# Two graph layers on 64 graphs: an order of their own for the weights and the first three graphs, Wv x aw, the constant and the bias sum on TensorE, turned square matrices in halves

## The chip, the cores and the metric

The kernel runs on one core of one Trainium2 chip. The metric is the device time of one execution in microseconds (us), and several executions are summed up by their median. The five engines named here are PE (TensorE), DVE (VectorE), ACT (ScalarE), POOL (GpSimd) and SP (SyncE, which only issues DMAs here). Each executes its own instructions in program order and waits for the others through semaphores.

## What is computed

There are 64 graphs of 256 nodes with 512 features, all in float32. Each graph goes through two layers, each with a layer norm, a relu and a residual sum around it.

```python
def _L0_gnn_ref(x, adj, W):
    deg = jnp.sum(adj, axis=-1, keepdims=True)
    agg = jnp.einsum('bij,bjf->bif', adj, x) / jnp.maximum(deg, EPS)
    cat = jnp.concatenate([x, agg], axis=2)
    return jax.nn.relu(jnp.einsum('bnf,of->bno', cat, W))

def _L1_gnn_ref(X, A, Wv, bv, aw, ab, Wk, bk):
    Xw = X @ Wv + bv
    sj, si = Xw @ aw[:d, 0], Xw @ aw[d:, 0]
    e = leaky_relu(sj[:, None, :] + si[:, :, None] + ab[0], negative_slope=0.2)
    alpha = A * jnp.exp(e)
    transition = alpha / (jnp.sum(alpha, axis=-1, keepdims=True) + 1e-12)
    H, Xk = 0, X
    for k in range(3):
        H = H + Xk @ Wk[k] + bk[k]
        Xk = jnp.einsum('bij,bjd->bid', transition, Xk)
    return jax.nn.relu(H)

h = jnp.maximum(_layernorm(x), 0.0);  x = x + _L0_gnn_ref(h, adj, W)
h = jnp.maximum(_layernorm(x), 0.0);  x = x + _L1_gnn_ref(h, adj, Wv, bv, aw, ab, Wk, bk)
```

Since `sj` and `si` are linear in X, the kernel never forms `Xw`. It computes once the two vectors v = Wv x aw (one for each half of aw, 512 numbers each) and the constant c = bv x aw + ab. The three rows of bk only ever occur as their sum.

## The kernel before

**Stages.** One graph is worked on in twelve stages (the list `ORDER`): `prepare` normalises x and scales the adjacency rows by the degree; `prepared` brings both turned; `aggregate` multiplies adjacency by h; `layer0` multiplies by W and adds to x; `turn1` normalises again and forms sj and si; `transition` builds the transition matrix; `moved`, `once`, `inner`, `turned1` and `outer` do layer 1 with it and store the result. `once` and `inner` need the turned transition matrix, and `inner` the weight Wk[2]. Large products are done with seven block products instead of eight (functions `spread`, `step`, `main`), so each needs sums of blocks: those of operands are made by `pool_op` on POOL, those of results by `copy` (ACT), `plus` and `minus` (DVE), which read PSUM. `main` has an order: step 5, then 1, 6 and 7, whose results pile up in one bank and are read between, and then 2, 3 and 4.

**The turned matrices.** `put` turns 32 by 32 blocks on DVE and stores them to DRAM in four DMAs, and `get` loads the whole turned matrix in one (`dan` and `ant` for the adjacency, `dtt` and `tt` for the transition, `dh` with `h0t` and `h1t` for h). Turned this way, the nodes of the two halves alternate in a row, so a half is read with a stride of two elements (8 bytes). For graphs 0 and 1 (adjacency and h) and the last two (transition) `flip_on_pe` turns on PE instead. In `spread` (function `turned`) `ant`, `tt` and their sums `sa` and `st` are the streamed operand of 128x128 products; in `outer` `tt` is the stationary one.

**Weights.** W, Wv, Wk, the biases and aw come in through SP. `weights_l0` turns W on PE, block by block, and ACT and DVE copy the blocks out in turn; `combine` makes the four further forms of a weight (1024-wide sums). `weights_l1` forms v on DVE, where Wv rows are multiplied by a broadcast aw with a running sum (line 607, ten such passes with those for c at line 626), sends it to DRAM (`dv`, line 610) and loads it back broadcast to all partitions (`v_sb`, line 612). The rows of bk are loaded broadcast and summed on DVE.

**Order.** Nothing is scheduled while the kernel runs. Every operation is recorded with `plan.add` (engine, a cost, what it reads and writes) and gets a due time from the table `AT` by stage and place in the stage, plus graph number times `TURN` and an entry of `SHIFT` for the first five and last five graphs. `emit` sorts each engine's operations by due time and writes them out; the costs do not enter the program. So an engine's queue is fixed, and an instruction that waits holds everything behind it. In the queue of SP loads and stores of all stages stand in one line.

**Closed stream.** After `inner` of graph 0 PE goes over to a repeating pattern, in which `outer` of one graph, `aggregate` and `layer0` of the graph two on, and `once` and `inner` of the graph between are interleaved. It is called the stream below.

Of the kernel before, what the change touches and what calls it, by code (L numbers as in the profile page):

```python
# [9 lines left out]
FP = mybir.dt.float32  # L10
BF = mybir.dt.bfloat16
AF = mybir.ActivationFunctionType
ALU = mybir.AluOpType
# [9 lines left out]
EDGE = 5  # L23
TURN = 41.62
AT = {
    "aggregate": (-3.8, 0.1, -3.6, 5.6, -18.4, -16.1, 2.2, -2.0, 2.2, 3.7, 9.3, 4.8, 4.4, 4.5, 5.0, 5.2, 14.3, 6.9, 13.8, 12.7, 10.0, 17.0, 11.4,
        18.9, 21.4),
    "first": (-579.1, -953.8, -882.7, -935.3, -1158.8, -875.5, -1084.4, -1059.4, -1372.1, -1103.9, -1257.7, -1270.0, -1219.5, -1116.0, -1213.5,
        -1124.5, -1222.8, -734.4, -1039.8, -990.3, -891.0, -945.8, -621.6, -565.5, -688.7, -847.3, -687.6, -419.9, -454.2, -670.2, -638.5, -533.2,
        -493.0, -301.0, -425.6, -241.2, -378.7, -391.4, -136.3, -308.3, -102.8, -3.0, -445.1),  # L30
    "inner": (79.0, 79.2, 80.3, 81.6, 79.5, 80.6, 80.7, 81.2, 82.3, 83.4, 83.7, 85.5, 86.5, 81.3, 86.1, 90.2, 104.7),
    "layer0": (5.8, 7.8, 11.6, 13.8, 6.8, 7.1, 14.9, 10.1, 10.2, 18.2, 13.6, 13.8, 15.2, 15.6, 16.8, 21.0, 27.0, 15.4, 16.4, 16.9, 17.5, 17.6, 18.4,
        22.0, 24.8),
    "loads": (-98.9, -113.0),
    "moved": (61.9, 69.8, 70.0, 71.6, 71.8),
    "once": (48.3, 49.8, 42.7, 60.1, 61.5, 65.2, 74.5, 70.0, 65.7, 66.7, 69.9, 70.9, 75.2, 70.4, 77.7, 76.5, 72.3, 77.8, 77.8, 78.3, 79.3),
    "outer": (81.8, 94.7, 105.9, 107.5, 84.9, 86.5, 92.3, 94.9, 96.6, 98.4, 98.5, 101.7, 102.6, 104.5, 106.4, 110.8, 109.6, 110.9, 111.5, 114.5,
        116.8, 117.1, 119.3, 120.1, 120.3, 125.6, 118.0, 118.6, 134.3, 139.3, 141.1, 145.8),
    "prepare": (-80.0, -76.6, -71.5, -69.0, -55.5, -53.4, -55.5, -20.1, -17.1, -104.1, -102.8, -91.0, -83.1, -82.8, -22.8, -22.9, -16.9, -16.1,
        -16.2, -17.5, -77.8, -47.6, -76.7, -52.4, -52.1),  # L40
    "prepare_early": (-499.7, -495.0, -519.1, -455.0, -518.6, -498.1, -241.7, -264.2, -416.8, -347.6, -281.6, -123.2, -111.2, -155.7),
    "prepared": (-12.9, -36.0),
    "prepared_early": (-136.7, -57.2, -102.3, -120.6, -45.1, -43.2, -73.0, -34.9),
    "transition": (33.1, 43.1, 53.6, 53.3, 53.8, 52.7, 50.1, 50.7, 50.6, 51.4, 51.5, 59.2, 59.4, 54.2, 58.0, 58.7, 55.9, 57.4),
    "transition_late": (28.6, 33.0, 57.8, 64.4, 61.5, 63.2, 59.1, 60.6, 60.9, 62.7, 64.3, 71.2, 71.5, 66.0, 69.8, 75.9, 91.9),
    "turn1": (24.0, 24.4, 26.7, 27.0, 31.9, 33.7, 29.4, 35.2, 35.5, 31.5, 32.5, 32.8, 41.4, 46.7, 50.6, 44.2, 46.3, 52.8, 52.0, 50.8, 51.3),
    "turned1": (79.0,),
    "weights": (-241.4, -226.2, -416.0, -218.0, -259.6, -285.0, -147.1, -112.2, -407.3, -158.3, -411.9, -155.5, -223.9, -130.8, -612.2, -212.8,
        -230.2, -181.7, -278.5, -209.9, -293.2, -203.1, -159.6, -81.9, -54.5, -36.5, -27.6, -3.8, -59.7, -38.2, 50.4, 51.5, 103.2, 18.1, -112.2,
        -238.5, 28.7, 43.7, -3.3, 3.7, 11.4, 21.4, 38.9, 9.0, 28.9, 12.6),  # L50
}
SHIFT = {(name, g): shift for g, row in {
    -5: {"aggregate": 0.5, "inner": 3.5, "layer0": 0.9, "loads": 5.6, "moved": 1.1, "once": 2.0, "outer": 3.9, "prepare": -1.3, "prepared": 15.2, "transition": 1.9, "turn1": -0.8, "turned1": 7.3},
    -4: {"aggregate": 0.9, "inner": 6.7, "layer0": 0.4, "loads": -2.2, "moved": 5.9, "once": 4.1, "outer": 4.8, "prepare": -1.2, "prepared": 12.3, "transition": 3.5, "turn1": -0.3, "turned1": 8.8},
    -3: {"aggregate": 3.5, "inner": 12.6, "layer0": 4.8, "loads": 7.5, "moved": 10.5, "once": 11.1, "outer": 9.9, "prepare": 0.7, "prepared": 20.2, "transition": 9.1, "turn1": 4.4, "turned1": -6.4},
    -2: {"aggregate": 9.6, "inner": 32.0, "layer0": 9.6, "loads": 0.8, "moved": 17.6, "once": 29.5, "outer": 37.1, "prepare": 5.9, "prepared": 18.0, "transition_late": 4.8, "turn1": 8.9, "turned1": 15.9},
    -1: {"aggregate": 16.4, "inner": 72.9, "layer0": 23.3, "loads": -1.2, "moved": 44.0, "once": 57.0, "outer": 78.7, "prepare": 9.1, "prepared": 30.2, "transition_late": 36.7, "turn1": 22.8, "turned1": 20.1},
# [66 lines left out]
def gnn_two_layers(ctx: ExitStack, tc: tile.TileContext, x, adj, w0, wv, bv, aw, ab, wk, bk, out):  # L124
# [39 lines left out]
    TURNED_A = buf("turneda", [N // Q, Q, NC], 2)  # L164
    H0T, H1T = buf("h0t", [FC, P, NC], 1), buf("h1t", [FC, P, NC], 1)
    S0, S1 = buf("s0", [4, 2, P], 1), buf("s1", [4, 2, P], 1)
    ANT, TT = buf("ant", [NC, P, NC], 1), buf("tt", [NC, P, NC], 2)
    SA, ST = buf("sa", [4, P], 1), buf("st", [4, P], 2)
    AG, ZG = buf("ag", [7, 2, P], 1), buf("zg", [7, 2, P], 1)
    QF = buf("qf", [7, half], 1)  # L170
# [538 lines left out]
```

## Time and profile before

| what | value |
|---|---|
| median of 3 runs | 2637.4 us (2636.27 to 2637.7) |
| the profiled execution's own time | 2636.42 us |
| its span (first to last instruction) | 2634.6 us |
| PE busy | 2572.8 us, 13520 matmul instructions |
| DVE, POOL, ACT busy | 1498.9, 1463.5, 696.2 us |
| mean granted TensorE clock | 0.99 |
| data moved by DMA | 300.48 MB, mean 114 GB/s |
| first and last store of a graph issued | 171.4 us, 2630.7 us |
| tt from DRAM, issue to landing, median | 2.9 us |

All times in the profile count from the start of the span. A product of float32 shows as several matmul instructions ("x4" for two products). A line of the timeline gives the start, the length, the engine, the source line, the operation and its tiles (output, then inputs) with the number of merged instructions, and in brackets the idle time before it and what ended that. Where the profile names a line of a helper (296, 308, 311, 259), the tiles tell which stage it is.

### The profile page before, as it was taken

The numbers are of one execution on the slowest core, as the hardware profiler recorded it, in microseconds if no ns is written. First come the engines' busy times: TensorE is split into PE (matmuls) and PEld (weight loads), VectorE is DVE, ScalarE is ACT, GpSimd is POOL, SyncE is SP. The second block draws the span as 40 slices with busy tenths as digits, with TensorE's granted clock in tenths as the row PEclk, the third lists the DMA queues.
The fourth block names the chain that finished last, engine by engine and source line by source line (L and its number), as shares of the span: only waits on it lengthen the run. The fifth ranks groups of instructions, "written<-read, shape, count | busy, mean of one in ns | idle before, by whom it ended". The sixth has DMA issues, their size and how long they took to land.

```text
span 2634.6 us, 39436 instructions
## 1 busy us (share of the span) xinstructions
PE 2572.8 (98%) x13520; PEld 2309.4 (88%) x13520; DVE 1498.9 (57%) x3686; ACT 696.2 (26%) x1680; POOL 1463.5 (56%) x2317
## 2 busy tenths in 40 slices
PE   5799999999999999999999999999999999999998
PEld 4688999999999999999999999999999998998887
DVE  5656556556556556556556556555555555556543
ACT  2223222222322322222222222222222222222221
POOL 4555555556556556556556556556556556556542
PEclk8799999999999999999999999999999999999999
DMA  5445445445445455354454455354355454445421
GB/s 177 88 112 129 102 120 129 102 120 129 100 122 125 103 124 128 97 126 122 101 128 121 100 125 127 98 128 120 101 128 121 99 130 120 102 114 125 103 67 50
DMA packets 578568, 300.48 MB, mean 114 GB/s; under 512 B 419904, under 2 KB 543808, under 8 KB 578368
## 3 DMA queue, kind: packets, MB, share of 16 engines
q1 hardware_dynamic: 578368, 297.97, 45.8%
q8 instruction: 107, 1.75, 0.3%
q14 instruction: 93, 0.76, 0.1%
HBM read 165.68 MB, written 132.19 MB: 113 GB/s over the span
## 4 chain that ended last, share of the span: by engine, by line
PE 95%; DMA 2%; DVE 2%; ACT 1%; issue 1%; POOL 0%; SPq 0%; DVEq 0%; ACTq 0%; POOLq 0%
PE bank L296 95%; DMA qf<-in_L_gnn_Wk_dram 1%; DMA dv<-vc 0%; DMA a<-in_adj_dram 0%; DVE z L471 0%; DMA lq<-in_L_gnn_Wk_dram 0%; ACT an L407 0%; DMA x<-in_L_gnn_W_dram 0%; DVE qf L311 0%; DVE z L607 0%; DMA dan<-turneda 0%; DVE stats L208 0%; ACT qf L308 0%; DVE x L398 0%; ACT si L453 0%
## 5 line engine op out<-in xcount | busy, mean ns | idle before, releaser
L296 PE MATMUL bank<-l,s 128*128 128x256 f32 x2048 | 527.6, 380 | 3.3 <-DVE bank L311 2.3
L296 PE MATMUL bank<-l,zg 128*128 128x256 f32 x1792 | 459.6, 379 | 0.0
L296 PE MATMUL bank<-l,ag 128*128 128x256 f32 x1792 | 451.9, 380 | 2.3 <-ACT ag L308 2.3
L259 POOL TENSOR_TENSOR zg<-zg 128x256 f32<-128x256 f32 x192 | 138.5, 734 | 562.7 <-ACT zg L308 546.9
L296 PEld LDWEIGHTS bank<-l,s 128*128 128x128 f32 x2048 | 380.1, 191 | 51.1 <-issue 2.6
L296 PE MATMUL bank<-lq,zg 128*128 128x256 f32 x1792 | 399.0, 379 | 2.5 <-DVE zg L311 1.4
L296 PEld LDWEIGHTS bank<-lq,zg 128*128 128x128 f32 x1792 | 339.7, 190 | 51.2 <-DVE zg L311 2.5
L296 PEld LDWEIGHTS bank<-l,ag 128*128 128x128 f32 x1792 | 341.6, 191 | 48.9 <-ACT ag L308 2.8
L296 PEld LDWEIGHTS bank<-l,zg 128*128 128x128 f32 x1792 | 330.5, 189 | 39.5
L259 POOL TENSOR_TENSOR ag<-ag 128x256 f32<-128x256 f32 x192 | 150.6, 785 | 364.3 <-DVE ag L311 225.5
L398 DVE SCALAR_TENSOR_TENSOR x<-bank,x 128x512 f32<-128x512 f32 x256 | 173.8, 679 | 94.1 <-PE bank L296 88.7
L296 PE MATMUL bank<-l,h1t 128*128 128x256 f32 x780 | 202.2, 382 | 5.2 <-ACT bank L308 3.3
L449 DVE SCALAR_TENSOR_TENSOR z<-h1n,v_sb 128x512 f32<-128x512 f32 x256 | 189.5, 740 | 12.6 <-ACT h1n L215 3.9
L296 PE MATMUL bank<-l,h0t 128*128 128x256 f32 x756 | 194.7, 380 | 1.1 <-DVE bank L383 0.6
L311 DVE TENSOR_TENSOR mq<-bank,mq 128x256 f32<-128x256 f32 x128 | 54.2, 424 | 225.7 <-PE bank L296 225.7
L208 DVE BATCH_NORM_STATS2 stats<-x 128x6 f32<-128x512 f32 x256 | 176.0, 688 | 2.3
L308 ACT COPY bank<-bank 128x256 f32<-128x256 f32 x128 | 45.7, 357 | 496.2 <-DVE bank L389 382.8
L308 ACT COPY zg<-bank 128x256 f32<-128x256 f32 x128 | 47.6, 372 | 471.9 <-DVE zg L311 299.9
L296 PEld LDWEIGHTS bank<-l,h1t 128*128 128x128 f32 x780 | 147.9, 197 | 20.6 <-ACT bank L308 3.7
L296 PEld LDWEIGHTS bank<-l,h0t 128*128 128x128 f32 x756 | 143.2, 196 | 15.4 <-ACT m L308 1.2
L296 PE MATMUL bank<-qf,st 128*128 128x256 f32 x512 | 152.3, 379 | 0.0
L259 POOL TENSOR_TENSOR s<-s,h1t 128x256 f32<-128x256 f32 x195 | 144.6, 743 | 0.1
(123 smaller groups left out, 4182.1 us busy)
## 6 DMA issues: line engine op xcount, KB each, us to landing
dh<-turned SPq DMA_DIRECT2D x504, 128.0 KB, 3.1
x<-in_x_dram SPq DMA_DIRECT2D x64, 512.0 KB, 4.3
h1t<-dh SPq DMA_DIRECT2D x64, 512.0 KB, 5.5
out_dram<-x SPq DMA_DIRECT2D x64, 512.0 KB, 3.8
h0t<-dh SPq DMA_DIRECT2D x62, 512.0 KB, 4.7
a<-in_adj_dram SPq DMA_DIRECT2D x64, 256.0 KB, 3.3
dan<-turneda SPq DMA_DIRECT2D x248, 64.0 KB, 4.2
ant<-dan SPq DMA_DIRECT2D x62, 256.0 KB, 2.8
```

What stands on the lines that cost most here:

```text
L208: add("DVE", 0.67, lambda c=c: nc.vector.bn_stats(st[:, c, :], s[:, c, :]), [f"{sk}.{c}"], [f"{stk}.{c}"])
L259: add("POOL", cost, lambda: getattr(nc.gpsimd, f)(to, p, q), reads, [write])
L296: nc.tensor.matmul(ps, lhs, rhs, start=start, stop=True, skip_group_check=True)
L308: add("ACT", 0.37, lambda: nc.scalar.copy(dst, bank[b][:, cols]), [f"bank{b}"], dkeys)
L311: add("DVE", 0.43, lambda: nc.vector.tensor_add(dst, bank[b][:, cols], other), [f"bank{b}"] + okeys, dkeys)
L398: add("DVE", 0.69, lambda c=c: nc.vector.scalar_tensor_tensor(t[:, c, :], bank[banks[1 + c]], 0.0, t[:, c, :], op0=ALU.max, op1=ALU.add), ...
L449: add("DVE", 0.85, lambda s=s, c=c: nc.vector.scalar_tensor_tensor(scr.rearrange("p c n -> p (c n)"), h[:, c, :], 1.0, v_sb[:, s, :], op0= ...
```

## The change

- **Order.** `AT` is a new table throughout, with two decimals. Graphs 0, 1 and 2 (`OWN = 3`) have due times of their own for every stage instead of a common table and a shift; the shifts remain for the last four graphs, and `moved` has a late form for the last two. `TURN` is the same. The costs in `add`, which emit nothing, are changed too. `warm` emits nothing, as `WARM` is 0.
- **Loads.** Graph 0's x comes in two halves, and its adjacency is the second load of all; W's four blocks follow, with graph 1's x and adjacency between them, then layer 1's weights.
- **v, c and the bias sum.** aw is loaded as 1024 single elements to a column per partition and spread by ACT to 128 columns; Wv is turned on PE (16 turns, copied out by ACT), and PE multiplies. The result is broadcast to all partitions as it comes. c is 8 products of one column, the bias sum one product with ones. The broadcast loads, the passes on DVE and the way through DRAM are gone.
- **Halves.** `ant` and `tt` hold the two halves of a row one after the other. The load goes to a new tile `raw`, and ACT copies it over (`even`). The turns on PE are copied straight into the new layout.
- **Engines.** For graphs 0 and 1 the sums for `ag`, `zg`, `qf`, `sa` and `st` go from POOL to DVE. Of W's blocks ACT copies twelve of sixteen instead of eight; ACT alone copies out the turned h.

```diff
-EDGE = 5
+EDGE = 4
+OWN = 3
+WARM = 0
...
-    ANT, TT = buf("ant", [NC, P, NC], 1), buf("tt", [NC, P, NC], 2)
+    ANT, TT = buf("ant", [NC, NC, P], 1), buf("tt", [NC, NC, P], 2)
+    RAW = buf("raw", [NC, P, NC], 2)
...
+    def even(raw, to):
+        (r, rk), (t, tk) = raw, to
+        add("ACT", 0.62, lambda: nc.scalar.copy(t, r.rearrange("p k n c -> p k c n")), [rk, rk + "'"], [tk, tk + "'"])
...
-                (nc.scalar.copy if c else nc.vector.tensor_copy)(t[:, :, :, c], pt[:, :n, :])
+                (nc.scalar.copy if c or width == F else nc.vector.tensor_copy)(t[:, :, :, c] if width == F else t[:, :, c], pt[:, :n, :])
...
     def pool_op(f, cost, to, p, q, reads, write):
-        add("POOL", cost, lambda: getattr(nc.gpsimd, f)(to, p, q), reads, [write])
+        if plan.graph < 2 and write[:2] in ("ag", "zg", "qf", "sa", "st"):
+            add("DVE", 0.45 if cost > 0.6 else 0.3, lambda: getattr(nc.vector, f)(to, p, q), reads, [write], port=True)
+        else:
+            add("POOL", cost, lambda: getattr(nc.gpsimd, f)(to, p, q), reads, [write])
...
     def left_of_t(tt, s):
-        a11, a12, a21, a22 = (t[:, k, :, c] for c in range(2) for k in range(2))
+        a11, a12, a21, a22 = (t[:, k, c] for c in range(2) for k in range(2))
...
-            get(N, of(D["an"], g), of(ANT, g))
+            get(N, of(D["an"], g), RAW[0])
+            even(RAW[0], of(ANT, g))
...
-            get(N, of(D["tt"], g), of(TT, g))
+            get(N, of(D["tt"], g), RAW[1])
+            even(RAW[1], of(TT, g))
...
-                        (nc.scalar.copy if oc % 2 else nc.vector.tensor_copy)(to[:, 2 * side : 2 * side + 2, (oc % 2) * P : (oc % 2 + 1) * P],
+                        (nc.vector.tensor_copy if side and kh else nc.scalar.copy)(to[:, 2 * side : 2 * side + 2, (oc % 2) * P : (oc % 2 + 1) * P],
...
-    def weights_l1():
+    def weights_l1(banks):
...
+        add("SP", 0.4, lambda: nc.sync.dma_start(awc, aw.rearrange("(s c p) o -> p s (c o)", p=P, s=2)), [], ["awc"], 3.5)
...
+        add("ACT", 1.1, lambda: nc.scalar.copy(awb, awc.unsqueeze(3).to_broadcast([P, 2, FC, P])), ["awc"], awbk)
+        for oc in range(FC):
+            b = next(banks)
+            def turn(b=b, oc=oc):
+                for c in range(FC):
+                    nc.tensor.transpose(bank[b][:, c * P : (c + 1) * P], wv_sb[c // 2][0][:, c % 2, oc * P : (oc + 1) * P], ident)
+            add("PE", 0.88, turn, ...)
+            add("ACT", 0.6, lambda b=b, oc=oc: nc.scalar.copy(wvt[oc][0], bank[b]), ...)
+        for s in range(2):
+            b = next(banks)
+            def product(b=b, s=s):
+                for oc in range(FC):
+                    matmul(bank[b], awb[:, s, oc, :], wvt[oc][0], oc == 0)
+            add("PE", 3.45, product, ...)
+            add("ACT", 0.6, lambda b=b, s=s: nc.scalar.copy(v_sb[:, s], bank[b]), [f"bank{b}"], [f"v{s}"])
...
+                matmul(bank[b][:, :1], awb[:, i // FC, i % FC, :], bvc[:, i % FC : i % FC + 1], i == 0)
...
+        add("PE", 0.9, lambda b=b: matmul(bank[b], ones, bk3, True), parts(Z[0][1]) + parts(Z[1][1]), [f"bank{b}"])
...
-                add("DVE", 0.85, lambda c=c, s=s: nc.vector.scalar_tensor_tensor(scr, wv_sb[c // 2][0][:, c % 2, :], 1.0, awf[:, s, :], op0=ALU.mult, ...
-        add("SP", 0.4, lambda: nc.sync.dma_start(DV.rearrange("s c p -> p (s c)"), vc.rearrange("p s c -> p (s c)")), ...
-        add("SP", 0.4, lambda: nc.sync.dma_start(v_sb.rearrange("p s f -> p (s f)"), ...
...
     def first():
-        load(0, "x")
+        for c in range(NC):
+            add("SP", 0.8, lambda c=c: nc.sync.dma_start(t[:, c, :], x[0, c * P : (c + 1) * P, :]), [], [f"{k}.{c}"], 3.0)
...
-                kind = name + ("_early" if g < 2 and name in ("prepare", "prepared") else "_late" if g >= G - 2 and name == "transition" else "")
-                plan.stage(kind, g, g if g < EDGE else g - G if g >= G - EDGE else None)
+                kind = name + (f"_{g}" if g < OWN else "_late" if g >= G - 2 and name in ("transition", "moved") else "")
+                plan.stage(kind, g, g - G if g >= G - EDGE else None)
```

## The prediction

> **What bounds the kernel now.** I began with the page's span and slices and then asked for busy time in four stretches.
>
> ```profile
> span 2634.6 us, 39436 instructions
> ...
> PE 2572.8 (98%) x13520; PEld 2309.4 (88%) x13520; DVE 1498.9 (57%) x3686; ACT 696.2 (26%) x1680; POOL 1463.5 (56%) x2317
> ...
> PEclk8799999999999999999999999999999999999999
> ```
> ```profile
> 0.00:120.00 120.00, 70.26 (x312) 57.22 (x312) 67.18 (x146) 27.37 (x63) 56.26 (x78) 0.79 0.48 138
> 120.00:200.00 80.00, 79.83 (x422) 71.44 (x421) 46.74 (x113) 22.15 (x55) 49.77 (x76) 1.00 0.43 103
> 200.00:2480.00 2280.00, 2279.54 (x12060) 2056.19 (x12060) 1321.91 (x3276) 618.28 (x1495) 1295.39 (x2069) 1.00 0.48 117
> 2480.00:2634.60 154.60, 143.20 (x732) 124.54 (x730) 63.10 (x153) 28.41 (x70) 62.08 (x96) 1.00 0.23 60
> ```
>
> After the first number each row gives length and then PE's busy time. From 120 to 2480 us TensorE is busy all the time at full clock, so nothing that frees another engine counts there. Only two things count: the spacing of matmuls, and the two ends. In the full-clock timeline a row of two products of 128x256 (x4, four instructions) is followed by the next 0.865 us later, so 216 ns an instruction; one of 128x128 is 111 ns where `sa` or `st` is streamed. One graph has 154 of the first and 56 of the second: 154 x 0.216 + 56 x 0.111 = 39.4 us, 64 graphs 2526, and with the turns on PE some 2532. The span is 102 us more. By the same spacing the first 120 us hold 49 us of matmul work, so 71 of the 102 are lost there, some 16 between 120 and 2480, and 15 in the last stretch.
>
> The timeline of PE shows the losses of the first stretch (start, length, then the idle time before and what ended it):
>
> ```profile
> 30.62 1.12 PE L246 MATMUL bank<-ident,an 128*128 128x128 f32 x4 [8.21 <-ACT h0t L252]
> ...
> 44.91 0.69 PE L246 MATMUL bank<-ident,an 128*128 128x128 f32 x2 [3.17 <-DVE h1t L252]
> 45.39 1.91 PE L296 MATMUL bank<-l,s 128*128 128x256 f32 x4
> ...
> 70.83 1.22 PE L296 MATMUL bank<-ant,h1n 128*128 128x128 f32 x4 [8.17 <-ACT mz L308]
> ...
> 102.71 1.22 PE L296 MATMUL bank<-tt,h1n 128*128 128x128 f32 x4 [3.53 <-DMA tt<-dtt]
> ```
>
> Who was late stands in the timelines of DVE and SP and in the chain:
>
> ```profile
> 28.36 0.69 DVE L624 TENSOR_TENSOR lq<-qf,lq 128x512 f32<-128x512 f32 x1 [6.24 <-DMA lq<-in_L_gnn_Wk_dram]
> 62.78 0.69 DVE L403 TENSOR_REDUCE deg<-a 128x2 f32<-128x512 f32 x1 [4.00 <-DMA a<-in_adj_dram]
> ```
> ```profile
> 46.94 8.56 DMA dv<-vc
> 55.51 0.34 SPq L612
> 55.90 6.85 DMA a<-in_adj_dram
> ```
>
> The first wait: DVE stood at a weight of layer 1 with graph 0's degrees behind it. The second: SP stood at the 8.56 us round trip of `dv`, with graph 2's adjacency behind it, and DVE's queue waited for that. `inner` of graph 0 ends and the closed stream begins at 117.47 in PE's timeline.
>
> **The change part by part.** The program order of each engine is fixed by the code, so I followed the new start by hand with the old rows' durations.
>
> *Loads.* In the first 30 us the DMA view gives 10.23 MB at 341 GB/s, with the first bytes after 2 us; so C MB have landed at about 2 + C/0.341. The new SP order brings x and adjacency of graph 0 (0.75 MB) at 4.2 us, two blocks of W at 7, both others with x and adjacency of graph 1 at 12.3, both halves of Wv (5.25 MB in all) at 17.4. Before, adjacency 0 came behind 3.75 MB.
>
> *Layer 0 of graph 0.* Degree and norm on DVE and POOL: 0.65 + 0.17 + 0.16 + 2 x 0.78 + 0.22 + 0.71 + 0.15 = 3.6, to 7.9; h0n on ACT 2 x 0.8, to 9.5. ACT then has h0t (2 x 0.6), four copies of W (0.37 each, the last behind the block that lands at 12.3) and ant, so `aggregate` can begin near 14.4. On PE Wv's turns stand inside it, so it waits for Wv until 18, and the form `l_5` (DVE, 1.22) ends at 19.3. I put the first step of `main` at 22.5 where the old one stood at 45.39. It took 16.2 us then; new between its steps are 16 turns of Wv and 12 of graph 1 (28 x 0.11), so 19.5: it ends at 42 (old 61.6).
>
> *v, constant, bias.* DVE loses ten passes over 512 columns (0.7 to 0.9), SP the broadcasts, the `dv` round trip and v's load (6.4 us to landing). PE gains 8 products of 512 columns (16 x 0.43 = 6.9 us), 16 of one column and one bias sum, about 9 us in all behind the turns. These lie in PE's idle time but in front of h1n(0), whose tile holds the spread-out aw: v and constant are done at 50.5, where h1n could have begun at 46.5. Price 4 us, against 68.2 for that h1n before.
>
> *Transition of graph 0.* From h1n to `once` by rows: 1.5 + two sums 1.5 + ds 2.8 + row 4.5 + four exponents 1.8 + max 0.7 + two products 0.9 + 0.75 + an 0.9 + turn 0.7 + dtt 1.8 + 2.4 + tt 2.9 + the new copy 0.65 = 23.8. The old stretch took 34.5 (68.2 to 102.71). I take 28.5, under half of the surplus of 10.7, as DVE's work between them is other than before (products at 2.5 us each under POOL's 1024-wide rows then); 24 and 34.5 are the ends. `once` starts at 79, and with the old 14.8 for `once` and `inner` the stream closes at 94. `aggregate` and `layer0` of graph 1, 15 us of PE, fit between 50 and 79. That is 23.5 us less than 117.5; with the favourable ends (no surplus, 5 us less in `main`'s interruptions and v) 84 (33 less), with the whole surplus and aw's load (next) 104 (13 less). I count 23.
>
> *aw's load.* It is SP's 24th issue, near 21 us, and writes 1024 single elements. The nearest row is `dv`, also 1024 elements of 4 bytes, 8.56 us: landed at 30. ACT's copy that spreads aw stands ahead of the bank copy of `main`'s first step, wanted at 26, so up to 4 us late. I take nothing, since `dv` goes to DRAM and this load comes from there, and keep 4 for the range. The Trainium skill, "DMA: Bandwidth & Descriptors", Rules for kernel authors, speaks against this form: a strided last dimension costs one descriptor per element. By that rule the 4 us would be in the sum (2607), by my reading of the row they are not (2603).
>
> *Contiguous squares.* In the stream, a row of `ant` or `tt` against plain 128x128 rows:
>
> ```profile
> 1211.94 0.61 PE L296 MATMUL bank<-st,hf 128*128 128x128 f32 x4
> 1212.38 0.62 PE L296 MATMUL bank<-tt,h1n 128*128 128x128 f32 x4
> 1212.85 0.60 PE L296 MATMUL bank<-st,hf 128*128 128x128 f32 x4
> ...
> 1231.54 0.72 PE L296 MATMUL bank<-ant,h0n 128*128 128x128 f32 x4
> 1232.10 0.60 PE L296 MATMUL bank<-sa,hf 128*128 128x128 f32 x4
> 1232.54 0.62 PE L296 MATMUL bank<-ant,hf 128*128 128x128 f32 x4
> ```
>
> `tt` takes 0.47 to the next row, `st` 0.44. The strided operand is streamed, so I put the difference down to it: `ant` and `tt` are streamed in six rows a graph, 0.017 each on average, 0.1 us, over 60 graphs 6 us less; the other end is nothing. The row at 1231.54 takes 0.56: it waits for the mz copy, which ACT starts late, behind two `si` (0.48). The new ACT order has `si` ahead of `mq`: 0.12 x 60 = 7 less at best, 0 at worst; I take 4.
>
> *What the squares' copies cost.* Two ACT copies of 512 columns a graph, 0.62 each (row of h1t<-bank). They stand after the last `bank` copy of layer 0, where ACT idles from 1206.9 to 1210.85 today; `tt`, issued at 1201.93, lands 2.9 to 3.7 later. POOL's first `st` moves from 1207.14 to about 1207.7, and PE wants it at 1211.94. Nothing, while the load lands before about 1209; after that each us late is a us of PE, since mz is queued behind. The adjacency copy has 27 us of slack. POOL sums moved to DVE for graphs 0 and 1, and ACT instead of DVE for W, are within the hand count.
>
> *The end* is ordered anew with the same instructions: 15 us lost, of which 6 are the final sum and store. I take 1.5 less, ends 5 less and 4 more.
>
> Sum: 2634.6 - 23 - 6 - 4 - 1.5 = 2600.1. Its execution took 2636.42, 1.8 over its span, and the median of three is 2637.4, another 1.0: 2603.
>
> **The rivals.**
> 1. Forecast, 0.60: 2603; its own range 2590 to 2616.
> 2. ACT is held by aw's load and the TensorE route to v is the new late one: the start gives 8, not 23. Speaks for it: strict queues, 8.6 us for such a load. Against: it would have to last to 40 us. 2637.4 - 8 - 11.5 = 2618. Chance 0.14.
> 3. The start is won, but the stream gains nothing and loses 0.1 us a graph to its new order: 2637.4 - 23 + 6 = 2620. For: the stride's share rests on 17 ns a row. Against: the order of PE in a period is almost the old one. 0.14. It holds also the case that the halves do not speed the streamed rows at all.
> 4. Slower: ACT's copy of tt waits in the queue for its load and mz behind it, in every graph. It needs tt to land 3.5 us later than now; from there 1 us a graph is 60 us, and 34/60 = 0.57 us a graph eats the gain. At 1.5 us: 2603 + 90 = 2693. For: loads under traffic took up to 7 us (row). Against: dtt's four issues stand a place earlier than before. 0.10.
> No change is left with 0.02.
>
> **How the numbers follow.** The time is rival 1's. The range 2588 to 2626 holds it with its bounds and rivals 2 and 3, and leaves out 4 and the extremes. Of three runs 0.05% lie between ends, so 0.2% (5 us) can be told. Faster 0.87, same 0.03, slower 0.10.
>
> **What would show it.** The start: PE's waits of 8 us gone, `once` near 79, TensorE's work of the first 120 us up by 30. The stream: `ant` and `tt` rows at 0.445 to the next, no 0.56. The squares: tt's copy beginning within 1 us of its load's landing, and no PE idle charged to mz. I am wrong if PE waits in the stream, or if `inner` of graph 0 ends after 110.

## The result and the profile after

The changed kernel takes 2598.32 us (median of four, 2597.91 to 2599.09) against 2637.36 for the kernel before, measured beside it: a ratio of 0.9853, 95% interval [0.9836, 0.987]. Its profiled execution took 2598.62 with a span of 2596.5, 38.1 less than the span before.

The page of the changed kernel, the lines that answer to those shown of before:

```profile
span 2596.5 us, 39394 instructions
...
PE 2563.3 (99%) x13570; PEld 2300.1 (89%) x13570; DVE 1522.4 (59%) x3687; ACT 791.4 (30%) x1822; POOL 1461.8 (56%) x2286
...
PEclk9999999999999999999999999999999999999999
```

The two squares' copies are most of the 95 us that ACT is busy longer (124 by about 0.65); neither ACT nor DVE is the bound. Busy time by stretch in the changed kernel (start:end, length, then PE, PEld, DVE, ACT, POOL, each with its instructions, granted clock, DMA share, GB/s):

```profile
0.00:120.00 120.00, 96.24 (x483) 78.47 (x484) 80.35 (x176) 43.18 (x98) 57.54 (x75) 0.94 0.53 140
120.00:200.00 80.00, 79.80 (x429) 71.54 (x428) 48.70 (x119) 25.61 (x59) 42.29 (x67) 1.00 0.47 116
200.00:2480.00 2280.00, 2279.49 (x12117) 2056.76 (x12116) 1348.18 (x3284) 701.93 (x1616) 1319.71 (x2077) 1.00 0.46 116
2480.00:2596.50 116.50, 107.80 (x546) 93.35 (x545) 45.12 (x108) 20.65 (x50) 42.29 (x67) 1.00 0.22 62
```

In the first 120 us PE is busy for 96.24 us instead of 70.26, and the granted clock is 0.94 instead of 0.79. Counted by the spacing of matmuls, as in the prediction, 83 us of work lie there instead of 49, and the loss is 37 instead of 71. Of the 71, by PE's busy time, 50 were idle and 21 were rows spaced wider than at full clock; of the 37 it is 24 and 13. So some 8 of the 34 us are rows that are no longer stretched, which the prediction doesn't tell from waits.

For the rest I compare the start of the first `tt` product of each graph in both traces. It lies 23.2 us earlier than before in graph 0, 18.8 in graph 1, 23.7 in graph 4, 24.6 in graph 10, 31.5 in graph 50, 34.3 in graph 61; the end of the span lies 38.1 earlier. So the start gave 23.2, the stream from graph 0 to 61 gave 11.1 (4.4 were lost in graph 1 and made good by graph 4; then 0.17 a graph), and the last stretch gave 3.8.

The start, from the timeline of PE in the changed kernel (start, length, instruction, then the idle time before and what ended it):

```profile
21.73 1.03 PE L351 MATMUL bank<-l,s 128*128 128x256 f32 x4
...
38.99 7.03 PE L351 MATMUL bank<-l,h1n 128*128 128x512 f32 x16
45.86 1.84 PE L351 MATMUL bank<-bvc,h1n 128*128 128x1 f32 x16
...
54.42 1.19 PE L351 MATMUL bank<-ant,hf 128*128 128x128 f32 x4 [2.89 <-DVE mz L369]
...
79.47 0.61 PE L351 MATMUL bank<-tt,h1n 128*128 128x128 f32 x4
...
93.90 1.03 PE L351 MATMUL bank<-l,s 128*128 128x256 f32 x4
```

The waits of 8 us are gone; after the first matmul the longest is 2.89. `main` of graph 0 begins at 21.73, v is formed on PE from 38.99 (the program names aw's spread columns `h1n`, after the tile that they lie in), `once` begins at 79.47 and `inner` ends at 93.90.

The stream, from the same timeline:

```profile
1201.23 0.61 PE L351 MATMUL bank<-ant,h0n 128*128 128x128 f32 x4
...
1202.54 0.61 PE L351 MATMUL bank<-sa,hf 128*128 128x128 f32 x4
1202.98 0.61 PE L351 MATMUL bank<-ant,h0n 128*128 128x128 f32 x4
1203.43 0.61 PE L351 MATMUL bank<-sa,hf 128*128 128x128 f32 x4
...
1222.06 0.61 PE L351 MATMUL bank<-tt,h1n 128*128 128x128 f32 x4
1222.50 0.61 PE L351 MATMUL bank<-st,hf 128*128 128x128 f32 x4
```

The `ant` row at 1202.98 is followed after 0.45, and so is the `tt` row at 1222.06; there is no 0.56. Over the stream an instruction of `ant` or `tt` takes 111 to 112 ns instead of 114 to 115. The copies that pay for it, from the timeline of ACT:

```profile
1178.04 0.36 ACT L363 COPY bank<-bank 128x256 f32<-128x256 f32 x1 [6.02 <-DVE bank L444]
1178.31 0.67 ACT L286 COPY tt<-raw 128x512 f32<-128x512 f32 x1
1178.87 0.67 ACT L286 COPY ant<-raw 128x512 f32<-128x512 f32 x1
1183.20 0.37 ACT L363 COPY mz<-bank 128x256 f32<-128x256 f32 x1 [3.66 <-PE bank L351]
```

Neither copy waits (no bracket), and ACT is idle for 3.66 us behind them before the next `mz`: they lie in a gap. The load for `tt` and the product that wants it, from the timelines of SP and PE:

```profile
1172.34 0.38 SPq L280 DMA_DIRECT2D raw<-dtt  x1
```
```profile
1182.55 0.61 PE L351 MATMUL bank<-tt,h1n 128*128 128x128 f32 x4
```

This load took 2.56 us (2.7 in the median), so it landed at 1174.9, 3.4 us before its copy and 7.65 before the product.

### The profile page after: what moved, and what is told of

Same layout as the page of the kernel before. It is cut to its first block, busy times and chain, and to the rows that moved or that the text cites. A ratio compares the mean times of both kernels' runs of the same rounds, so it can differ in the third digit from the quotient of the medians.

```text
span 2596.5 us, 39394 instructions
## 1 busy us (share of the span) xinstructions
PE 2563.3 (99%) x13570; PEld 2300.1 (89%) x13570; DVE 1522.4 (59%) x3687; ACT 791.4 (30%) x1822; POOL 1461.8 (56%) x2286
## 4 chain that ended last, share of the span: by engine, by line
PE 97%; DMA 1%; DVE 1%; issue 0%; SPq 0%; ACT 0%; POOL 0%; DVEq 0%; ACTq 0%; POOLq 0%
PE bank L351 97%; DMA qf<-in_L_gnn_Wk_dram 0%; DMA x<-in_L_gnn_W_dram 0%; DVE z L505 0%; DMA awc<-in_L_gnn_aw_dram 0%; DMA dh<-turned 0%; PE bank L298 0%; POOL zg L314 0%; DMA ds<-sj 0%; SPq L274 0%; DVE bank L366 0%; DVE zg L366 0%; PE bank L613 0%; DVE z L527 0%; DVE stats L255 0%
## 5 line engine op out<-in xcount | busy, mean ns | idle before, releaser
L351 PE MATMUL bank<-l,ag 128*128 128x256 f32 x1792 | 461.7, 380 | 0.4 <-ACT ag L363 0.4
L314 POOL TENSOR_TENSOR ag<-ag 128x256 f32<-128x256 f32 x186 | 141.2, 772 | 187.4 <-ACT ag L363 156.7
L314 POOL TENSOR_TENSOR st<-tt 128x128 f32<-128x128 f32 x124 | 56.6, 456 | 285.5 <-ACT tt L286 267.8
L505 DVE SCALAR_TENSOR_TENSOR z<-h1n,v_sb 128x512 f32<-128x512 f32 x256 | 208.7, 815 | 9.6 <-PE bank L351 4.0
L351 PEld LDWEIGHTS bank<-l,h0t 128*128 128x128 f32 x756 | 143.5, 196 | 14.2 <-DVE bank L438 0.7
L363 ACT COPY qf<-bank 128x256 f32<-128x256 f32 x128 | 47.7, 373 | 333.8 <-DVE qf L366 182.6
```

Of the source, the lines that this page charges most:

```text
L314: add("POOL", cost, lambda: getattr(nc.gpsimd, f)(to, p, q), reads, [write])
L351: nc.tensor.matmul(ps, lhs, rhs, start=start, stop=True, skip_group_check=True)
L363: add("ACT", 0.37, lambda: nc.scalar.copy(dst, bank[b][:, cols]), [f"bank{b}"], dkeys)
L505: add("DVE", 0.83, lambda s=s, c=c: nc.vector.scalar_tensor_tensor(scr.rearrange("p c n -> p (c n)"), h[:, c, :], 1.0, v_sb[:, s, :], op0= ...
```

## The experiments

Each kernel was timed beside the kernel before, whose medians in these calls were 2636.6 to 2637.8. Ratios are to the kernel before. "First `tt`" is the start of the first `tt` product of graph 0, 102.71 in the kernel before and 79.47 in the changed one.

### The halves alone, on the kernel before

```diff
-    "moved": (61.9, 69.8, 70.0, 71.6, 71.8),
+    "moved": (61.9, 68.9, 69.8, 70.0, 71.6, 71.8),
+    "moved_late": (61.9, 69.8, 70.0, 71.6),
-    "prepared": (-12.9, -36.0),
+    "prepared": (-12.9, -36.0, -14.3),
-    ANT, TT = buf("ant", [NC, P, NC], 1), buf("tt", [NC, P, NC], 2)
+    ANT, TT = buf("ant", [NC, NC, P], 1), buf("tt", [NC, NC, P], 2)
...
```

> The kernel before with one part of the change alone: ant and tt in contiguous halves, written by an ACT copy from a raw tile, all else in its old order (the copies stand behind the last bank copy of layer 0). Prediction's step: 24 streamed 128x128 products of ant and tt a graph go from 115 to 111 ns, 0.1 us a graph over 60 graphs, so 6 us less: 2631, start and end unchanged, and the ACT copies cost nothing. Rival 3: the halves do not speed the streamed rows: 2637, rows of ant still at 115 ns. Rival 4: the copies make mz late: over 2640, with TensorE idle before rows that wait for mz.

Measured: 2662.38 us, ratio 1.0096 [1.0082, 1.011]. Slower by 25 us, beyond the 2640 of rival 4, though not by the way that it names. The first `tt` product is later than before by 14.2 us in graph 5, 13.9 in graph 10 and 12.1 in graph 50, then by 24.4 in graph 60 and 27.5 in graph 63. So in the undisturbed inner graphs it gains 0.045 us a graph, and everything is lost at the two ends. There the shifts of the due times (`SHIFT`) put the copy in another place of ACT's queue. The timeline of this kernel, all engines, near the end:

```profile
2392.29 0.37 ACT L315 COPY qf<-bank 128x256 f32<-128x256 f32 x1 [2.98 <-DVE qf L318]
2392.55 0.51 ACT L414 ACTIVATE an<-a,deg 128x256 f32<-128x256 f32 x1
2392.97 0.64 ACT L241 COPY ant<-raw 128x512 f32<-128x512 f32 x1
2393.69 0.87 POOL L266 TENSOR_TENSOR sa<-ant 128x128 f32<-128x128 f32 x2 [7.70 <-ACT ant L241]
...
2396.09 2.07 PE L303 MATMUL bank<-l,s 128*128 128x256 f32 x4 [4.63 <-POOL s L266]
```

The copy of `ant` stands behind a `qf` copy, for which ACT waits 2.98 us on DVE. POOL, in its order at `sa`, idles for 7.70 until the copy is done; the sum `s` stands behind `sa`, and PE idles for 4.63 until it comes; it is such sums that PE waits for after 2300 us (9.0 of 18.1 us; 6.8 in all in the kernel before), and not `mz`. This run measures a badly placed copy, not the layout; so the next one keeps the ends as they were.

### The halves in the inner graphs only

```diff
+    def inside(g):
+        return EDGE <= g < G - EDGE
...
+            if inside(g):
+                get(N, of(D["an"], g), RAW[0])
+                even(RAW[0], of(ANT, g))
+            else:
+                t, k = of(ANT, g)
+                get(N, of(D["an"], g), (strided(t), k))
```

> The kernel before with the contiguous halves in graphs 5 to 58 only; in the five graphs at each end, which have due times of their own, the old strided layout and order stay, so that ACT's two copies stand behind the last bank copy everywhere. If the run with the halves in all graphs lost its 25 us to copies in wrong places of ACT's order at the two ends, this one is faster than before: prediction's step says 0.1 us a graph, 54 graphs, 5.4 us less, 2631.5; by the period seen in that run (0.045 us less) 2.4 us less, 2634.5. Rival: the copies cost time in every graph: 2637 or more.

Measured: 2634.10 us, ratio 0.999 [0.9981, 0.9999]. From graph 10 to 50 the first `tt` comes 1.84 us earlier, 0.046 a graph. The layout is worth about 2.8 us over 60 graphs in the old order, half of the 6 that I had put down to it. In the first halves run the rows show where some of it goes: the first of the two `ant,h0n` rows is shorter, but the second still takes 0.55, as it ends when ACT's `mz` copy comes. From the first row to the one after the second it takes 2.33 us instead of 2.35 (medians of the inner graphs).

### The changed kernel without the halves

```diff
-    "moved": (60.74, 69.13, 70.92, 73.26, 76.68, 73.57),
+    "moved": (60.74, 70.92, 73.26, 76.68, 73.57),
-    ANT, TT = buf("ant", [NC, NC, P], 1), buf("tt", [NC, NC, P], 2)
+    ANT, TT = buf("ant", [NC, P, NC], 1), buf("tt", [NC, P, NC], 2)
...
```

> The changed kernel with ant and tt loaded straight into the old strided layout, without the raw tiles and ACT's two copies a graph; all other orders as changed. Prediction's step: 6 us more than the changed kernel, 2604, rows of ant and tt back at 115 ns. Rival: the layout does nothing and the stream's gain is order alone: 2598. Second rival: ACT's copies cost something in the stream, then less than 2598.

Measured: 2602.85 us, ratio 0.987 [0.9855, 0.9885], 4.5 more than the changed kernel. The period grows by 0.065 us a graph (3.9 over 60), and `ant` and `tt` are back at 115 ns. So with `mz` out of the way the layout gives more, but not 0.1: 24 instructions a graph by 3 to 4 ns are 0.07 to 0.1. From start to start the rows of `ant` and `tt` gain 0.08 us a graph between the two traces, and the 24 instructions of `sa,hf` and `st,hf` beside them take 111.6 ns with the halves and 110.5 without, which gives 0.03 of it back.

### The two `si` ahead, on the kernel before

```diff
-    "turn1": (..., 41.4, 46.7, 50.6, 44.2, ...),
+    "turn1": (..., 41.4, 40.9, 41.0, 44.2, ...),
```

> The kernel before with only the two si activations moved in ACT's order, from in front of the mz copy to in front of the an copies; nothing else changes. Prediction's step: the row that takes 0.56 us to the next one falls to 0.45, 0.11 us a graph, 60 graphs, so 7 us less: 2630. Rival: the 0.11 us comes back at a later row or was never the mz copy's: 2637, and the period of 39.68 us a graph stays.

Measured: 2630.27 us, ratio 0.9974 [0.9964, 0.9984]. The span is 7.3 us shorter and the period 39.56 instead of 39.68. That is 0.12 us a graph, 0.10 from the row of 0.56 and 0.02 from the row ahead of it, all that this wait had to give. The timeline of PE of this kernel at that place:

```profile
1227.31 0.61 PE L296 MATMUL bank<-sa,hf 128*128 128x128 f32 x4
1227.75 0.62 PE L296 MATMUL bank<-ant,h0n 128*128 128x128 f32 x4
1228.22 0.60 PE L296 MATMUL bank<-sa,hf 128*128 128x128 f32 x4
```

The strided row now takes 0.47 to the next where it took 0.56: the wait is gone, and what is left is the stride.

### Two queues at the start, on the kernel before

```diff
-        ..., -59.7, -38.2, 50.4, 51.5, 103.2, 18.1, -112.2,
-        -238.5, 28.7, 43.7, ...),
+        ..., -59.7, -11.0, 50.4, 51.5, 103.2, 18.1, -112.2,
+        2.0, 28.7, 43.7, ...),
```

The one number lets DVE's difference of Wk, which waited for its load, stand behind graph 0's degrees; the other puts v's load behind graph 2's adjacency in SP's queue.

> The kernel before with two moves of order at the start: on DVE the difference of layer 1 weights that waited for its load at 28.36 us goes behind graph 0's degrees, and on SP the load of v goes behind adjacency and x of graph 3. If the two 8 us waits were queue order, as the prediction says, aggregate of graph 0 begins some 5 us earlier and the wait at 70.8 us shrinks; v still comes by the old DRAM round trip, so the first product with tt comes 5 to 12 us earlier: 2626 to 2632. Rival (the old route to v bounds the start, and the queues do not): under 2 us less, 2636 or more.

Measured: 2628.33 us, ratio 0.9968 [0.9956, 0.9981]. First `tt` at 94.65, 8.1 earlier; from graph 1 on it stays at 9.0. The timeline of PE of this kernel:

```profile
61.55 1.22 PE L296 MATMUL bank<-ant,h1n 128*128 128x128 f32 x4 [5.82 <-ACT mz L308]
...
94.65 1.22 PE L296 MATMUL bank<-tt,h1n 128*128 128x128 f32 x4 [4.00 <-DMA tt<-dtt]
```

Of two waits of 8 us the first is down to 1.28, and the second to 5.82. So the queues alone give 9 of the 23.

### Graph 0's adjacency later, in the changed kernel

```diff
 "first": (...
-        -151.49, -59.03, ...),
+        -26.0, -59.03, ...),
```

> The changed kernel with one load moved: adjacency of graph 0 from second to tenth place of SP's order, behind 4.25 MB as in the kernel before. Prediction's step (early loads let aggregate of graph 0 begin near 14.4): it lands near 15, aggregate begins near 19 instead of 14.8, and since TensorE has work without a gap from 20 to 47 us the delay stays: 3 to 4 us more, 2601 to 2602. Rival: the weight turns fill the time and nothing is lost: 2598.

Measured: 2610.11 us, ratio 0.9899 [0.9885, 0.9912]; first `tt` at 89.50, 10.0 later than in the changed kernel, and 10.3 at the end. I had expected 3 to 4. The timelines of DVE and PE of this kernel show what I had not counted:

```profile
16.98 0.69 DVE L458 TENSOR_REDUCE deg<-a 128x2 f32<-128x512 f32 x1 [16.98 <-DMA a<-in_adj_dram]
...
17.99 0.67 DVE L255 BATCH_NORM_STATS2 stats<-x 128x6 f32<-128x512 f32 x1
```
```profile
21.87 1.97 PE L298 MATMUL bank<-ident,h0n 128*128 128x128 f32 x8 [12.05 <-ACT h0n L262]
```

The degrees stand first in DVE's queue, so with the adjacency x's statistics wait too, which need no adjacency, and after them h0n and PE. In the kernel before this adjacency landed about as late (16.3 us, here 16.96), but the first statistics of x began at 11.93, ahead of the degrees: so the 10 us are what a late adjacency costs in the new order, not what the early load gained over the old one.

### v on VectorE again, in the changed kernel

The eight passes with a running sum, the two for c, the round trip through `dv` and the broadcast load are put back; the turns of Wv, the products and aw's spread are left out.

```diff
+            for s in range(2):
+                add("DVE", 0.85, lambda c=c, s=s: nc.vector.scalar_tensor_tensor(scr, wv_sb[c // 2][0][:, c % 2, :], 1.0, awf[:, s, :], ..., accum_out=vc[:, s, c : c + 1]), ...)
+        add("SP", 0.4, lambda: nc.sync.dma_start(DV..., vc...), ...)
+        add("SP", 0.4, lambda: nc.sync.dma_start(v_sb..., DV...), ["dv"], ["v"], 6.0)
```

> The changed kernel, but v and the constant are computed the old way: ten DVE passes, v to DRAM and back broadcast to all partitions; the turns of Wv, its products and the constant leave TensorE. Five passes stand where DVE idles before 27 us, three before the second bank sum of layer 0. TensorE gets 10.5 us less to do. Prediction's step (v on TensorE costs 4 us in front of h1n of graph 0): passes done near 37, v back 15 us later at 52, 3 us later than the first row sum begins in the changed kernel, so 2600 to 2602. Rival 2: TensorE's route is the late one, then less than 2598. Second rival: DVE's passes push layer 0 of graph 0: 2605 or more.

Measured: 2601.42 us, ratio 0.9866 [0.9851, 0.9881]; first `tt` at 82.25, 2.8 later than in the changed kernel, and as much to the end. From the timelines of DVE and PE of this kernel:

```profile
27.88 2.72 DVE L670 SCALAR_TENSOR_TENSOR mq<-l,turned 128x512 f32<-128x512 f32 x1
...
54.34 1.23 DVE L506 SCALAR_TENSOR_TENSOR z<-h1n,v_sb 128x512 f32<-128x512 f32 x1 [1.43 <-DMA v_sb<-dv]
```
```profile
35.43 2.07 PE L352 MATMUL bank<-l,h0t 128*128 128x256 f32 x4 [5.92 <-DVE bank L439]
...
51.99 1.23 PE L352 MATMUL bank<-ant,h1n 128*128 128x128 f32 x4 [5.94 <-ACT mz L364]
```

The passes, with POOL's sums beside them, make PE wait 5.92 us, and v comes so late that the first row sum begins at 54.34 instead of 49.41. But it then takes 1.23 us instead of 2.79, and PE has the turns and products of Wv less to do; 2.8 are left, as the expectation had it. They hold for this place of the passes in DVE's queue; another was not tried. So forming v on TensorE is the smallest of the three parts of the start that were measured: 9.0, 10.0 and 2.8. That they add to 21.8 of 23.2 is no proof, as they were measured in different kernels, and the 10.0 is not a gain over the kernel before.

### The load of tt later, in the changed kernel

```diff
-    "moved": (60.74, 69.13, 70.92, 73.26, 76.68, 73.57),
+    "moved": (64.2, 69.13, 70.92, 73.26, 76.68, 73.57),
```

> The changed kernel with one move in SP's order: the load of tt goes behind the next adjacency load, the output store and the next x load, so that in the stream it is issued some 6.5 us later (1178.9 instead of 1172.3 in the profiled frame) and lands near 1181.7, where ACT's copies of tt and ant would otherwise run at 1178.3. Rival 4's rule in the prediction (from a landing 3.4 us ahead of the first row with tt, each us late is a us of TensorE in every graph): the landing is 2.5 us beyond that point, 60 graphs, 150 us more, 2748. By the rows of the changed kernel: copies at 1181.7 to 1182.8, tt wanted at 1182.55, its first sum at 1183.0, mz at 1183.2: at most 0.5 us a graph, 2598 to 2628.

Measured: 2705.42 us, ratio 1.0257 [1.024, 1.0274], 107 us more than the changed kernel, between the two figures that I had expected (2748 and at most 2628). This is the prediction's fourth rival, save that PE waits for the copy of `tt` itself and not for an `mz` queued behind it. The timelines of SP, ACT and PE of this kernel:

```profile
1224.84 0.36 SPq L280 DMA_DIRECT2D raw<-dtt  x1
```
```profile
1228.64 0.65 ACT L286 COPY tt<-raw 128x512 f32<-128x512 f32 x1 [5.00 <-DMA raw<-dtt]
```
```profile
1229.34 0.71 PE L351 MATMUL bank<-tt,h1n 128*128 128x128 f32 x4 [1.38 <-ACT tt L286]
```

The copy is taken up as soon as the load lands, and the product when the copy ends. Here the load was issued at 1224.84 and took 3.8 us (median over the graphs 3.7 instead of 2.7). PE wanted the product at 1229.34 - 1.38 = 1227.96, so by this row a landing 0.7 us ahead of that, the copy's length, would have let this product start in time. In the changed kernel the load lands 7.65 us ahead, so it has some 6.9 in hand, where the prediction had given 3.5. Past the point it is dearer than the prediction had it: 1.4 us too late cost 2.1 a graph (from graph 10 to 50 the period is 41.64 us instead of 39.51), of which 1.4 is this wait (76.0 us in 53 such waits); the rest I have not followed. Where exactly the loss begins wasn't tried.

### The changed kernel with the end of before

The last five graphs get the old table and shifts (`EDGE = 5`, stages named `old_...`).

> The changed kernel with the due times of the kernel before for the last five graphs (halves kept, their copies behind the last bank copy); where the two tables meet some instructions are taken out of due order. Prediction's step: the new end is worth 1.5 us, so 2600. By the traces of both kernels, whose gap grows by 4 us from graph 60 to the last matmul: 2602. Rival: the seam or the copies' places at the end cost far more, 2605 to 2620, with TensorE waiting in the last 200 us.

Measured: 2625.11 us, ratio 0.9959 [0.9947, 0.9972]; 26.8 more than the changed kernel, past even the rival's 2620. The first `tt` is later by 4.7 us in graph 58, 13.3 in graph 59 and 29.8 in graph 62. The loss begins where the two tables meet, for instance in the timeline of PE:

```profile
2443.42 1.13 PE L362 MATMUL bank<-l,s 128*128 128x256 f32 x4 [3.02 <-POOL s L325]
```

So the run measures the seam between two orders, and what the new end is worth by itself stays open.

### An own version: v's consumers freed

In the changed kernel, the first row sum after v is held up by two things that it doesn't need, which the timelines of DVE, PE and POOL of the changed kernel show:

```profile
49.41 2.79 DVE L505 SCALAR_TENSOR_TENSOR z<-h1n,v_sb 128x512 f32<-128x512 f32 x1 [4.03 <-PE bank L351]
```
```profile
48.18 1.12 PE L351 MATMUL bank<-z,z 3*128 3x512 f32 x2
```
```profile
49.31 2.35 POOL L593 TENSOR_TENSOR l<-l,qf 128x1024 f32<-128x1024 f32 x1
```

The first half of h1n was there near 47.8, but the row sum writes a tile `z` that holds the ones of the bias sum until that (48.18 to 49.30) has read them. Then it takes 2.79 us instead of the usual 0.69, while POOL's 1024-wide sum runs. And h1n itself began at 47.02 only: aw's spread columns lay in its tile, and both copies of v stood ahead of it in ACT's queue. The edit: aw's columns in another tile, the bias sum first, each half of v waited for by itself, its copies around h1n, POOL's sums for Wk behind the row sums, and four operations of graph 1 a place earlier.

```diff
-        awb, awbk = flat(H1[0][0])..., parts(H1[0][1])
+        awb, awbk = TURNED[0][0]..., parts(TURNED[0][1])
-                    [f"{hk}.{c}", "v"], ...
+                    [f"{hk}.{c}", f"v{s}"], ...
+            add("POOL", 0.2, lambda: nc.gpsimd.tensor_scalar(held, sj[:, 1], 0.0, None, op0=ALU.add), [sjk + ".00", ...], ["held"])
...
```

> The changed kernel with its start put right where the trace shows waits: the spread aw lies in the tile of the turned h1n, so h1n of graph 0 no longer waits for the products of v; the copies of v stand around h1n and each row sum waits for its half of v only; the bias sum stands ahead of the products, so that the row sums no longer wait for its operand tile; POOL's 1024-wide sums of layer 1 wait until the row sums are done; two ag sums and two bank operations of graph 1 stand a place earlier. If the chain from h1n of graph 0 to its first product with tt sets the start, the row sums begin near 45.5 instead of 49.4 and run 2 us shorter: 4 to 6 us less, 2592 to 2594. Rival: the chain only moves into the waits of layer 0 of graph 1: less than 2 us, 2596 to 2598.

Measured: 2590.96 us (2590.26 to 2591.25), ratio 0.9824 [0.981, 0.9839]: 7.4 us faster than the changed kernel, more than the 4 to 6 expected. First `tt` at 72.68, 6.8 earlier, and 7.1 at the end. The timelines of DVE and POOL of this version:

```profile
45.33 0.69 DVE L501 SCALAR_TENSOR_TENSOR z<-h1n,v_sb 128x512 f32<-128x512 f32 x1 [0.23 <-ACT h1n L258]
45.95 0.08 DVE L501 DVE_READ_ACCUMULATOR z<-h1n,v_sb 128x1 f32 x1
46.14 0.69 DVE L501 SCALAR_TENSOR_TENSOR z<-h1n,v_sb 128x512 f32<-128x512 f32 x1
```
```profile
48.70 4.69 POOL L593 TENSOR_TENSOR l<-l,qf 128x1024 f32<-128x1024 f32 x2
```

The row sums take 0.69 and are done when POOL begins, and the wait of 2.89 on PE is gone.

### Two further versions

Both only move due times in the start of the first own version. `own_start_2` brings the row of sums in `transition_0` and graph 1's results forward and puts others back; `own_start_3` keeps to graph 1's results and `moved_0`. In short, of the second and then of the third:

```diff
-    "transition_0": (28.76, 33.82, ..., 55.72, 56.65, 58.43, 59.05, 59.82, ..., 67.47, ...),
+    "transition_0": (28.76, 28.78, ..., 49.6, 49.62, 49.64, 49.66, 49.68, ..., 50.7, ...),
-    "prepared_2": (1.30, -40.98, -7.65),
+    "prepared_2": (1.30, -40.98, -3.54),
...
```
```diff
-    "moved_0": (76.33, 81.06, 83.24, 84.14, 87.66, 89.23),
+    "moved_0": (76.33, 81.06, 79.0, 79.1, 87.66, 89.23),
-    "layer0_1": (..., 22.07, ..., 25.78, ...),
+    "layer0_1": (..., 17.83, ..., 18.38, ...),
...
```

> The kernel of the run own_start with the waits that are left before the first product with tt taken on in the same way: SP issues the load of row as soon as ds can have landed and not behind two other transfers; DVE does the maximum, the two products and the sums of the attention rows before it turns squares of graphs 2 and 3; the copy of m and the two ag copies of graph 1 stand a place earlier on ACT, two bank operations and two st sums a place earlier on DVE. If DMA and DVE order in that chain is what is left, the first product with tt begins 2 to 4 us earlier than at 72.7: 2587 to 2589. Rival: TensorE's own chain through layer 0 of graph 1 is the bound by now: 2590 to 2592.

Measured: 2595.09 us, ratio 0.9838 [0.9825, 0.9851], 4.1 slower than the version before it and outside both ranges expected. The store of the turned transition matrix was issued at 67.23 instead of 63.38, and the copy of `tt` waited, by ACT's timeline:

```profile
74.67 0.65 ACT L282 COPY tt<-raw 128x512 f32<-128x512 f32 x1 [3.99 <-DMA raw<-dtt]
```

> The kernel of the run own_start with only four of the second run's moves, none of which puts work in front of the chain of graph 0: ACT's copy of m in front of the first exponent of graph 0 and the second ag copy in front of the second h0n; on DVE the second bank sum of layer 0 of graph 1 in front of two batch statistics, and two st sums of graph 0 in front of a sum of graph 1. Each takes away a TensorE wait that the trace of own_start shows (1.58, 0.8, 0.8 and 1.46 us). As ACT's copy of tt ends at 71.5 there and the first product with tt began at 72.7, at most 1.2 of the first three can be had, and 1.46 of the last: 2 to 2.7 us less, 2588 to 2589. Rival: they delay the chain of graph 0 as the second run did: 2591 or more.

Measured: 2591.18 us (2589.77 to 2592.79), ratio 0.9826 [0.9812, 0.9839]. In its profiled execution the first `tt` comes at 71.41, 1.3 earlier, but the medians are equal: not told apart from the first own version, which remains the fastest.

## Why the prediction was right

The forecast was 2603, and 2598.3 was measured. By spans it was 2600.1 against 2596.5; the other 1.1 is what I had added around the span (2.9, where it was 1.8). The mechanisms are those of the prediction, but that the sums of the start and of the stream came out within 1.1 us each is luck: in both, errors of their terms cancel. By its steps:

**The start, 23: measured 23.2.** The two ends of it are right, 79 and 94 against 79.47 and 93.90, but the middle by two errors that cancel. `main` began at 21.73 and the products of v behind it at 38.99: 17.3 us instead of the 19.5 counted, ending three sooner than the 42. The mis-sized term is the old stretch of 16.2 us that the prediction carried over. Its first two rows were spaced 1.7 us or more instead of 0.865, by PE's timeline of the kernel before:

```profile
45.39 1.91 PE L296 MATMUL bank<-l,s 128*128 128x256 f32 x4
47.10 1.91 PE L296 MATMUL bank<-l,ag 128*128 128x256 f32 x4
```

The granted clock from 45.39 to 49.10 was 0.50; over all of `main` in the changed kernel, from 21.73 to 38.99, it is 1.00. At the spacing of full clock the two rows would have been 1.7 us shorter, most of the 2.2. h1n began at 47.02, 3.5 before the 50.5. From h1n to `once` I had allowed 28.5; it took 32.5. The surplus over that lay in the row sums' waits for `z` and for POOL: in the own version, which takes these away, the same way is 28.2 (44.48 to 72.68).

**The price of v on PE, 4 us.** In the own version, with aw's columns elsewhere and v's copies around h1n, h1n begins 2.5 us earlier (44.48), so 2.5; another 1.6 (47.8 to 49.41) are the row sum's wait for the bias sum, which the prediction had among PE's work but not as a wait of DVE's.

**aw's load.** Landing was put at 30, after the 8.56 of `dv`; it took 5.5 and landed at 27.7. From the timeline of ACT in the changed kernel:

```profile
27.72 1.04 ACT L658 COPY h1n<-awc 128x1024 f32<-128x1024 f32 x1 [0.80 <-DMA awc<-in_L_gnn_aw_dram]
28.67 0.37 ACT L363 COPY bank<-bank 128x256 f32<-128x256 f32 x1
```

The copy holds ACT up for 0.80 and the bank copy behind it until 28.67; PE waited 1.25 us for that at 29.09. So it cost 1.25 of the 0 to 4 that I had given it, and `main` still ended sooner than counted. The Trainium skill, "DMA: Bandwidth & Descriptors", Rules for kernel authors, says that such a load is split into one descriptor per element. The trace agrees with the split (1283 packets under 512 bytes between 22.2 and 28 us) but shows no price for it here: a 256 KB load of an adjacency, issued 0.4 us later, took 5.6 us in the same traffic. The 4 us that the prediction put beside that rule were too many.

**The stream, 10: measured 11.1, with both terms mis-sized.** "Contiguous squares" was 6 and measured 3 to 4: the six rows gave 0.08 us a graph instead of 0.1, the rows of `sa` and `st` beside them lost 0.03, which the prediction had not counted, and in the old order the wait for `mz` took another part. The row of 0.56 was put at 4 and gave all of its 7. The errors cancel.

**The squares' copies, 0: right.** They lie in ACT's gap. The sign given for that, a copy within 1 us of its load's landing, did not show: the load lands 3.4 us ahead of its copy, as ACT takes the copy up behind a bank copy that waits. The fourth rival's condition, "3.5 us later than now", was too strict: it took a limit 3.4 us ahead of the first product, where the late run points to 0.7, while the landing itself stayed where it was (7.4 us ahead in the kernel before, 7.65 now). Its mechanism, but for `mz`, and its price (60 us and more per us) are what that run shows.

**The end, 1.5: measured 3.8.** Of it 2.5 are PE's waits in the last stretch (6.6 before, 4.1 after, by their brackets); where the rest comes from I have not followed, and the experiment on it measured the seam instead.

**The rivals.** Rival 2 needed ACT to be held until 40 us; it was held until 28.7. Rival 3 needed the stream to give nothing; it gave 11. One reading under "Loads" is wrong: before, adjacency 0 stood behind 4.5 MB and not 3.75 (graph 1's stands ahead of it), and landed at 16.3; the sum doesn't rest on it.

## What to carry to other kernels

In a kernel whose engines run in program order, look at each start-up wait for what else stands behind the waiting instruction: here two changed due times gave 9 us of 23, and a late adjacency cost 10 because the degrees made of it stood first in VectorE's queue. The same small copy was free in the stream and cost PE 4.6 us at the end of the run with the halves alone, by what it was queued behind; it must be placed for the first and last rounds as well as for the steady ones. When a new path shares a tile with an old one, the tile's next writer and reader wait: freeing two such tiles, with GpSimd's sums moved behind the row sums, was worth another 7 us. And durations carried over from an old trace carry its clock with them: two rows at a granted clock of 0.50 were 1.7 us too many.

## What the hardware showed that I had not expected

- A 512-wide row sum on VectorE with two operands in SBUF took 0.69 us alone, and 2.79 while a 1024-wide sum ran on GpSimd: it began at 49.41 and ended at 52.20, half a us behind GpSimd's end at 51.66. Others beside GpSimd's sums took 1.0 to 2.7. The Trainium skill, "GPSIMD Engine Reference", section 1. Specifications, says that its SBUF interfaces are shared with VectorE and contended by instructions with two SBUF inputs; the rows agree, and they give the size.
- The stride of 8 bytes in a streamed float32 operand costs 3 to 4 ns on an instruction of 128 columns (114 to 115 against 111 to 112).
- The same load of 256 KB took 2.7 or 3.7 us (medians) by its place in the period.
- 1024 single elements of 4 bytes took 8.6 to 8.8 us from SBUF to DRAM, with next to no other traffic. The other way they took 5.5 us, no longer than a 256 KB load issued beside them (5.6).
